# Eight-tile blocks, moves on two queues, and a new order of the first loads in a conditional residual kernel

## The chip, the cores and the metric

The kernel runs on one core of a Trainium2 chip. The metric is the device time of one execution in microseconds (us). A core has five engines with instruction streams of their own: TensorE (PE, matrix products), VectorE (DVE), ScalarE (ACT), GpSimd (POOL) and SyncE (SP, which here only starts transfers). Each works through its stream in order, and they wait for each other through semaphores. Transfers (DMA) are started by an engine's queue and carried out by 16 DMA engines beside the five.

## The reference

For x of 4 x 1024 x 512 (four rows of 1024 positions), cond of 4 x 256, W of 1536 x 512 and b of 512, all float32:

```python
hidden = concatenate([cond, cond], axis=-1)                    # 4 x 512
x_mean = mean(x, axis=1, keepdims=True)                        # 4 x 1 x 512
fused = concatenate([x, x_mean * ones_L, hidden[:, None, :] * ones_L], axis=-1)
out = x + relu(einsum('bld,do->blo', fused, W) + b)            # 4 x 1024 x 512
```

W thus has three parts of 512 rows: one is multiplied with x, one with the mean of x over a row, one with the condition. The last two and b give one vector of 512 for each row, called the bias below. It can only be finished when the whole row of x has been seen.

## The kernel before

x is cut into 32 tiles of 128 positions, eight to a row. A tile's product needs x transposed, and float32 accuracy is kept by splitting both sides into a rounded part `hi` and a rest `lo`: hi x w_hi, lo x w_hi and hi x w_lo, for each of four chunks j of 128 input columns. That is 12 products of 128x512 a tile (`product`, L565).

Row 0 is transposed by PE itself (`turn`, L329; the units in BY_PE). Rows 1 to 3 are worked in blocks of four tiles, called z4 to z9, and go another way:

- `mix` (L311): DVE transposes 32x32 squares of a loaded block, four instructions i for four tiles, into a buffer `n`.
- `shuffle` (L321): 16 transfers inside SBUF, one for each pair (i, q), carry the squares from n to their place in `z`. These are the moves inside SBUF. SP issues all of them.
- `split_hi` (L353): ACT rounds z into `hi` and sums it up beside; `split_lo` (L365): DVE or POOL takes the rest.

The bias of row r: the sums of all its `hi` give `total` (L444), four `mean_term` (L465) on DVE add up w_mean times the totals in PSUM on top of the condition's part (`weigh` L448 on ACT, `add_term` L453 on POOL), then acc_hi (L472), acc_lo (L476), and two products with a matrix of 1/L on PE, `pb` (L483), spread the sum over all partitions; `bias_copy` (L487) takes it out on ACT.

A tile ends in one of three ways. Tiles under KEEP are copied out of PSUM by ACT and get bias, relu and x later on POOL, ACT, POOL (L580, L583, L586). Others get the bias on DVE out of PSUM (L580), relu on ACT, x on POOL. Tiles from EARLY on in a row have the bias put into PSUM before the product (`preload`, L553) and need one DVE instruction at the end (L590). Then SP stores them (L595). Five PSUM banks take turns for the tiles.

The order of the work on every engine is written out before it runs by a planner (`Plan`). Each operation has a cost on each engine that may do it, dependences, and a due time; at each step the operation that can start first and is due first is taken. SEED, SPREAD and SHIFT disturb the due times. What the planner emits is fixed in the program, and so is what stands behind what on each queue. The tile framework guards the transfers of SP's queue with eight counters that take turns: a transfer is issued only when the one eight places earlier has landed.

Buffers come from pools: seven blocks of 1 MB for x and parts of W (X_BUFS), two units of `n` (N_BUFS), two of `z`, twelve pieces of `hi` and `lo`. A load of x into a buffer waits until the block that held it is finished. The first loads, SP's from 0.7 us on, are a tile of x, half of W's first part, a tile of x, the other half, and then the large ones; cond is loaded by POOL's queue after b (L253). PE transposes cond (`turn_cond`, L428) at the head of its stream.

Of the kernel before, what the change touches and what calls it, by code (L numbers as in the profile page):

```python
# [18 lines left out]
class Plan:  # L19
# [15 lines left out]
    def run(self, seed=None, spread=1.0, shift={}):  # L35
# [19 lines left out]
        while ready:  # L55
            could = []
            for key, deps in ready.items():
                costs, names, _, _, _, lag = self.ops[key]
                if deps is None:
                    deps = ready[key] = [self.done[d] for d in names if d[0] != "issued"]  # L60
                    sent = [self.done[d][0] for d in names if d[0] == "issued"]
                    self.sent[key] = max(sent, default=0.0)
                options = []
                for engine, cost in costs.items():
                    start = max(self.free[engine], self.sent[key])
                    if self.ops[key][4]:
                        start = max(start, self.landed[-self.LANES])
                    for end, by in deps:
                        start = max(start, end if by == engine else end + self.HANDOVER + lag)
                    options.append((start + cost, start, engine))  # L70
                could.append((*min(options)[1:], due[key], key))
            first = min(could)
            start, engine, _, key = min(
                (t for t in could if t[1] == first[1] and t[0] <= first[0] + self.PATIENCE),
                key=lambda t: (t[2], t[0]),
            )
            del ready[key]
            costs, _, _, _, moves, _ = self.ops[key]
            end = start + costs[engine]
            self.log.append((start, engine, key, start - self.free[engine]))  # L80
            self.free[engine] = end
            if moves:
                self.line = max(self.line, start + self.ISSUE) + moves
                self.done[key] = (self.line + self.SETTLE, None)
                self.done["issued", key] = (end, engine)
                self.landed.append(self.line + self.SETTLE)
            else:
                self.done[key] = (end, engine)
            for u in users.get(key, ()):
                missing[u] -= 1  # L90
                if not missing[u]:
                    ready[u] = None
# [9 lines left out]
def kernel(  # L102
# [20 lines left out]
    S_BUFS = 12  # L123
    O_BANKS = 5
    N_BUFS = 2
    Z_BUFS = 2
    X_BUFS = 7
    O_BUFS = 7
    KEEP, PARKED = 5, 1.4
    EARLY = (99, 14, 20, 28)  # L130
    SINGLE = 2
    TERMS = 3
    N_WARM = 5
    SEED, SPREAD, SHIFT = 4710, 1.0, {
        "z": 2.0, "turn": -5.6, "stored": -16.3, "lo": 3.7, "acc_lo": 2.1, "acc_end": -3.2,
        "relu": 1.8, "finished": -0.1, "freed": 5.6, "preload": -3.1, "bias": 1.7, "w_lo": 7.2,
        "sh": -0.2, "acc_hi": -0.3, "added": -3.1, "mix": 1.8, "total": -2.1, "turn_cond": -2.2,
        "ones": 3.6, "x": -1.0, "hi": -1.4, "sum": -4.3, "product": 2.2, "copy_cond": -1.7,
        "w_hi": -0.8, "acc": -2.1, "weigh": 0.1, "mean": -5.0, "b_row": -2.4,
    }  # L140
    STEP, START, TURN = 2.81, 5.5, 0.48
# [18 lines left out]
    plan = Plan({"pe": 1.2 + 0.43 * N_WARM, "dve": 1.3, "act": 4.3, "pool": 3.9, "sp": 3.4})  # L160
# [8 lines left out]
    units += [(r, k, G) for r in range(1, B) for k in range(0, NK, G)]  # L169
# [6 lines left out]
    for u, (r, k0, n) in enumerate(units):  # L176
        pieces += [(u, tuple(range(J)))] if n == 1 else [(u, (j,)) for j in range(J)]
    piece_of = {(u, j): c for c, (u, js) in enumerate(pieces) for j in js}
# [10 lines left out]
    c_sb = const.tile([B, H], F32, name="c_sb")  # L189
    b_sb = const.tile([P, D], F32, name="b_sb")  # L190
# [25 lines left out]
    load_w(0, slice(0, J // 2))  # L216
    load_x(0, 1, 1)
    load_w(0, slice(J // 2, J))
    table_warm = const.tile([P, 1], F32, name="table_warm")
    nc.scalar.activation(table_warm, ones, AF.Relu)  # L220
    plan.given.update({("x", 0, 0): 3.6, ("w", 0): 4.7, ("w", 1): 4.7, ("x", 0, 1): 5.4, ("w", 2): 7.2, ("w", 3): 7.2})
    plan.line0 = 6.6
    plan.landed0 = [0.0] * 4 + [3.6, 4.7, 5.4, 7.2]
# [13 lines left out]
    for v in LOADS:  # L237
        if v == ("w_mean",):
            load(v, MB, [], -9, lambda e, _: load_w(1))
        elif v == ("cond",):  # L240
            load(v, MB, frees[v], -9, lambda e, _: load_cond())
        elif v == ("x", 0):
            load(("x", 0, 2), MB / 2, [], -9, lambda e, _: load_x(0, 2, 2))
        else:
            paced = [("mix", unit_of[divmod((v[1] - 2) * G, NK)], i) for i in range(NQ)] if v[1] > 3 else []
            load(v, MB, frees[v] + paced, -9 if v[1] < 4 else at(v[1] * G) - 22, lambda e, _, g=v[1]: load_x(g))
# [6 lines left out]
    nc.gpsimd.dma_start(out=c_sb, in_=cond)  # L253
# [39 lines left out]
    for j in range(J):  # L293
        plan.add(("w_hi", j), {"dve": 0.46} if not j else {"act": 0.65}, [("w", j)], 3 + 0.7 * j,
                 lambda e, _, j=j: split_w_hi(e, j))
        plan.add(("w_lo", j), {"dve": 0.72}, [("w_hi", j)], 4 + 0.7 * j,
                 lambda e, _, j=j: nc_of[e].tensor_tensor(
                     w_lo[:, j, :], w_x[:, j, :], w_hi[:, j, :].bitcast(F32), ALU.subtract))
# [7 lines left out]
    def mix(u, i):  # L306

        r, k0, n = units[u]
        if u not in ns:
            ns[u] = npool.tile([P, NQ, n * J * Q], F32, tag="n", name=f"n{u}")  # L310
        nc.vector.transpose(  # L311
            ns[u][:, i].rearrange("p (k j t) -> p k j t", k=n, j=J),
            xs[first_tile[u] // G][:, k0 % G : k0 % G + n].rearrange("p k (j i c) -> p i k j c", j=J, i=NQ)[:, i],
        )

    def shuffle(e, u, i, q):

        if u not in zs:
            zs[u] = zpool.tile([P, NQ, G * J * Q], F32, tag="z", name=f"z{u}")
        m = units[u][2] * J * Q  # L320
        nc_of[e].dma_start(out=zs[u][i * Q : (i + 1) * Q, q, :m], in_=ns[u][q * Q : (q + 1) * Q, i, :m])  # L321

    def turn(c):
        u, js = pieces[c]
        n = units[u][2]
# [8 lines left out]
    def turned(c):  # L334
        u, js = pieces[c]
        n = units[u][2]
        if u in BY_PE:
            return xT[c][:, : n * len(js) * P]
        v = zs[u][:, :, : n * J * Q].rearrange("p q (k j t) -> p j k q t", k=n, j=J)
        return v[:, js[0]]  # L340

    def like(c, v):
        u, js = pieces[c]
        v = v[:, : units[u][2] * len(js) * P]
        return v if u in BY_PE else v.rearrange("p (k q t) -> p k q t", q=NQ, t=Q)

    def split_hi(c):
        u, js = pieces[c]
        r = units[u][0]
        s = units_of_row[r].index(u)  # L350
        hi[c] = spool.tile([P, G * P], F32R, tag="hi", name=f"hi{c}")
        lo[c] = spool.tile([P, G * P], F32R, tag="lo", name=f"lo{c}")
        nc.scalar.activation(  # L353
            like(c, hi[c]), turned(c), AF.Copy,
            accum_out=sums[:, r, js[0], s : s + 1] if len(js) == 1 else None,
        )

    def add_up(c):
        u, js = pieces[c]
# [4 lines left out]
    def split_lo(e, c):  # L364
        nc_of[e].tensor_tensor(like(c, lo[c]), turned(c), like(c, hi[c]).bitcast(F32), ALU.subtract)  # L365

    SHUFFLE = {"sp": 0.45}
    PAIRS = ((0, 0), (2, 2), (0, 1), (2, 3), (0, 2), (2, 0), (0, 3), (2, 1))
    ring = []
    for n, u in enumerate(by_z):  # L370
        r, k0, m = units[u]
        early = min(at(first_tile[u]), at(EARLY[r]) - 5)
        room = [("sh", by_z[n - N_BUFS], i, q) for i in range(NQ) for q in range(NQ)] if n >= N_BUFS else []
        into = [("lo", c) for c in range(len(pieces)) if pieces[c][0] == by_z[n - Z_BUFS]] if n >= Z_BUFS else []
        for s, i in enumerate((0, 2, 1, 3)):
            plan.add(("mix", u, i), {"dve": 0.17 * m + 0.02}, [("x", first_tile[u] // G)] + room, early - 14 + 0.9 * s,
                     lambda e, _, u=u, i=i: mix(u, i))
        for s in range(2):
            for v, (i, q) in enumerate(PAIRS):
                plan.add(("sh", u, i + s, q), SHUFFLE, [("mix", u, i + s)] + into, early - 12 + 3.6 * s + 0.45 * v,  # L380
                         lambda e, _, u=u, i=i + s, q=q: shuffle(e, u, i, q), moves=0.055 * m, lag=0.3)
    for c, (u, js) in enumerate(pieces):
        r, k0, n = units[u]

        ahead = max(0.0, at(first_tile[u]) - at(EARLY[r]) + 1.2 + 3.4 + 0.4 * js[0])
        need = (at(first_tile[u]) if u > 1 else 4.5 + 2 * first_tile[u]) + 0.7 * js[0]
# [17 lines left out]
        if c >= S_BUFS:  # L404
            v, js_v = pieces[c - S_BUFS]
            deps.append(("product", first_tile[v] + units[v][2] - 1, js_v[-1]))
# [5 lines left out]
        if u not in BY_PE:  # L412
            costs = {"dve": 0.2 + 0.14 * w, "pool": 0.1 + 0.33 * w}
        plan.add(("lo", c), costs, [("hi", c)], need - 2.2 - ahead * 0.5, lambda e, _, c=c: split_lo(e, c))
# [35 lines left out]
    def add_term(r, n):  # L450
        if not n:
            conds[r] = small.tile([P, D], F32, tag="cond", bufs=B, name=f"cond{r}")
# [48 lines left out]
    for r in range(B):  # L501
        need = at(EARLY[r]) - 1.2
        for j in range(J):
            deps = [key for c, (u, js) in enumerate(pieces) if units[u][0] == r and j in js
# [4 lines left out]
        for n in range(KH):  # L509
            i = order.index((r, n))  # L510
            deps = [("add_cond", n), ("copy_cond",), ("b_row",)] + ([("term", *order[i - TERMS])] if i >= TERMS else [])
            if i:
# [42 lines left out]
    def product(t, j, h=None, some=range(3)):  # L555
        r, k = divmod(t, NK)
        u = unit_of[r, k]
        p = piece_of[u, j]
        c = pieces[p][1].index(j) * units[u][2] + k - units[u][1]
# [38 lines left out]
    for i, (t, h) in enumerate(halves):  # L598
# [11 lines left out]
        for j in range(J):  # L610
            c = piece_of[u, j]
# [67 lines left out]
```

## Time and profile before

| what | value |
|---|---|
| median of 3 runs | 136.48 us (135.6 to 136.68) |
| the profiled execution | 136.09 us, of which 134.3 us are the span from the first to the last instruction |
| mean granted clock of PE | 0.936 |
| PE busy | 107.7 us (80%), 454 instructions |
| DVE, ACT, POOL busy | 72.8 (54%), 56.0 (42%), 61.8 us (46%) |
| moves inside SBUF | 96 of 64 KB, 2.0 us from issue to landing |
| loads of x | 7 of 1 MB, 8.5 us to landing; 2 of 256 KB, 3.5 us; 1 of 512 KB, 6.8 us |
| chain that ended last | SP's queue 24%, PE 22%, DMA 20%, DVE 19% |

The times come from one profiled execution. An engine's name with a q (SPq) is its instruction sequencer, which is where the issue of a transfer shows. In the groups of instructions a row gives line, engine, operation and tiles, then the busy time, the mean of one, and the idle time of the engine just before them with what ended it. The 40 slices are 3.36 us long each, and their digits are tenths.

### The profile page before, as it was taken

What the parts mean: (1) busy time and instruction counts of PE and PEld (TensorE: products, weight loads), DVE (VectorE), ACT (ScalarE), POOL (GpSimd) and SP (SyncE); (2) the same over time, 40 slices, a digit from 0 to 9 for tenths busy, and PEclk for the clock granted to TensorE, in tenths of its full rate; (3) what the DMA queues carried; (4) which work ended last, traced back from release to release, by engine and by line L of the source; (5) the groups of instructions that cost most, each with busy time, mean ns of one, the idle gap of its engine ahead of it and who ended that gap; (6) DMA issues with size and microseconds to landing.
All of it is one profiled execution on the core that took longest, in us unless ns stands there. A gap on an engine that the chain in (4) does not pass through costs nothing.

```text
span 134.3 us, 1590 instructions
## 1 busy us (share of the span) xinstructions
PE 107.7 (80%) x454; PEld 84.3 (63%) x454; DVE 72.8 (54%) x127; ACT 56.0 (42%) x128; POOL 61.8 (46%) x56
## 2 busy tenths in 40 slices
PE   6039999999999970069999992999980999699990
PEld 1038888878868850057778881788750687488780
DVE  1026949994098029998199059882220907772230
ACT  4006377765296057040786071672002507186000
POOL 7140070999239974925369568068000007408600
PEclk9999999999999999555999999589999689999999
DMA  3999994144493459576566688974458750002841
GB/s 126 339 391 390 389 386 173 39 100 111 94 364 98 111 150 312 148 234 216 153 210 195 211 282 274 397 237 101 107 191 276 245 147 16 0 0 79 328 158 62
DMA packets 15288, 26.32 MB, mean 196 GB/s; under 512 B 2348, under 2 KB 2608, under 8 KB 15280
## 3 DMA queue, kind: packets, MB, share of 16 engines
q1 hardware_dynamic: 15216, 26.22, 60.4%
q8 instruction: 3, 0.05, 0.2%
q14 instruction: 5, 0.04, 0.1%
q0 software_dynamic: 64, 0.01, 0.0%
HBM read 11.54 MB, written 8.39 MB: 148 GB/s over the span
## 4 chain that ended last, share of the span: by engine, by line
SPq 24%; PE 22%; DMA 20%; DVE 19%; issue 6%; POOL 3%; ACT 3%; DVEq 0%; ACTq 0%; POOLq 0%
SPq L321 20%; PE po_None L565 16%; DMA z<-n 11%; DVE acc L465 6%; DVE lo L365 5%; DVE n L311 5%; DMA x<-in_x_dram 5%; DMA c_sb<-in_cond_dram 4%; SPq L595 4%; PE xT L329 2%; ACT hi L353 2%; PE po L565 2%; POOL o L586 1%; PE pb L483 1%; PE pw L259 1%
## 5 line engine op out<-in xcount | busy, mean ns | idle before, releaser
L565 PE MATMUL po_None<-w_hi,hi 128*128 128x512 f32 x124 | 51.6, 419 | 4.0 <-ACT hi L353 4.0
L565 PE MATMUL po_None<-w_hi,lo 128*128 128x512 f32 x124 | 51.2, 415 | 0.3 <-DVE lo L365 0.2
L565 PE MATMUL po_None<-w_lo,hi 128*128 128x512 f32 x124 | 50.9, 414 | 0.0
L586 POOL TENSOR_TENSOR o<-o,x 128x512 f32<-128x512 f32 x22 | 29.2, 1350 | 21.6 <-ACT o L583 21.0
L565 PEld LDWEIGHTS po_None<-w_hi,hi 128*128 128x128 f32 x124 | 25.1, 203 | 10.8 <-ACT hi L353 4.4
L353 ACT ACTIVATE hi<-z 128x512 fp32r<-128x512 f32 x24 | 14.8, 620 | 35.6 <-DMA z<-n 35.6
L565 PEld LDWEIGHTS po_None<-w_hi,lo 128*128 128x128 f32 x124 | 24.6, 198 | 6.9 <-DVE lo L365 1.1
L565 PEld LDWEIGHTS po_None<-w_lo,hi 128*128 128x128 f32 x124 | 24.7, 199 | 5.9
L365 DVE TENSOR_TENSOR lo<-z,hi 128x512 fp32r<-128x512 f32 x17 | 15.1, 932 | 13.3 <-ACT hi L353 13.3
L365 POOL TENSOR_TENSOR lo<-z,hi 128x512 fp32r<-128x512 f32 x7 | 8.8, 1288 | 20.9 <-ACT hi L353 20.9
L311 DVE STREAM_TRANSPOSE n<-x 128x512 f32<-128x512 f32 x24 | 15.2, 681 | 1.0 <-DMA x<-in_x_dram 1.0
L583 ACT ACTIVATE o<-o 128x512 f32<-128x512 f32 x22 | 13.0, 622 | 6.1 <-DVE o L580 6.0
L590 DVE SCALAR_TENSOR_TENSOR o<-po_None,x 128x512 f32<-128x512 f32 x9 | 6.1, 689 | 11.4 <-PE po_None L565 9.2
L580 DVE TENSOR_TENSOR o<-po_None,bias 128x512 f32<-128x512 f32 x17 | 11.0, 676 | 1.9 <-ACT bias L487 1.7
L483 PE MATMUL pb<-acc_hi,mean 128*128 128x512 f32 x4 | 2.2, 548 | 12.3 <-DVE acc_lo L476 12.3
L465 DVE SCALAR_TENSOR_TENSOR acc<-w_mean,tot,acc 128x512 f32<-128x512 f32 x15 | 11.3, 753 | 0.5
L444 DVE TENSOR_REDUCE tot<-sums 128x1 f32<-128x4 f32 x16 | 2.4, 150 | 14.9 <-ACT hi L353 14.9
L353 ACT ACTIVATE hi<-xT 128x512 fp32r<-128x512 f32 (+1 forms) x10 | 5.1, 510 | 12.7 <-PE xT L329 12.7
L483 PEld LDWEIGHTS pb<-acc_hi,mean 128*128 128x128 f32 x4 | 0.8, 212 | 13.6 <-DVE acc_lo L476 13.6
L580 POOL TENSOR_TENSOR o<-o,bias 128x512 f32<-128x512 f32 x5 | 6.9, 1396 | 5.0 <-ACT bias L487 5.0
L365 DVE TENSOR_TENSOR lo<-xT,hi 128x512 fp32r<-128x512 f32 (+1 forms) x10 | 5.6, 582 | 3.3 <-ACT hi L353 3.3
L453 POOL TENSOR_TENSOR cond<-b_sb,term 128x512 f32<-128x512 f32 x4 | 5.2, 1301 | 3.6 <-ACT term L448 3.6
(51 smaller groups left out, 82.8 us busy)
## 6 DMA issues: line engine op xcount, KB each, us to landing
out_dram<-o SPq DMA_DIRECT2D x31, 256.0 KB, 2.2
x<-in_x_dram SPq DMA_DIRECT2D x7, 1024.0 KB, 8.5
z<-n SPq DMA_DIRECT2D x96, 64.0 KB, 2.0
w_x<-in_L_cond_W_dram SPq DMA_DIRECT2D x2, 512.0 KB, 5.0
w_mean<-in_L_cond_W_dram SPq DMA_DIRECT2D x1, 1024.0 KB, 11.2
w_cond<-in_L_cond_W_dram SPq DMA_DIRECT2D x1, 1024.0 KB, 13.0
x<-in_x_dram SPq DMA_DIRECT2D x2, 256.0 KB, 3.5
x<-in_x_dram SPq DMA_DIRECT2D x1, 512.0 KB, 6.8
```

The lines of the kernel that those rows point to most:

```text
L311: nc.vector.transpose(ns[u][:, i].rearrange("p (k j t) -> p k j t", k=n, j=J), xs[first_tile[u] // G][:, k0 % G : k0 % G + n].rearrange("p ...
L321: nc_of[e].dma_start(out=zs[u][i * Q : (i + 1) * Q, q, :m], in_=ns[u][q * Q : (q + 1) * Q, i, :m])
L353: nc.scalar.activation(like(c, hi[c]), turned(c), AF.Copy, accum_out=sums[:, r, js[0], s : s + 1] if len(js) == 1 else None,)
L365: nc_of[e].tensor_tensor(like(c, lo[c]), turned(c), like(c, hi[c]).bitcast(F32), ALU.subtract)
L453: nc.gpsimd.tensor_tensor(conds[r], conds[r] if n else bL, terms[r, n], ALU.add)
L465: nc.vector.scalar_tensor_tensor(acc[r], w_mean[:, j, :], scale, acc[r], ALU.mult, ALU.add)
L565: nc.tensor.matmul(po, lhsT=v[p][:, c], rhs=m[:, j, cols(h)], start=(i == 0 and not preloaded(t)), stop=(i == 3 * J - 1), skip_group_check ...
L580: nc_of[e].tensor_tensor(o, o if t < KEEP else bank(t), biases[t // NK], ALU.add)
L583: nc.scalar.activation(outs[t], outs[t], AF.Relu)
L586: nc_of[e].tensor_tensor(outs[t], outs[t], x_tile(t), ALU.add)
L590: nc.vector.scalar_tensor_tensor(o_tile(t)[:, d], bank(t, h), 0.0, x_tile(t)[:, d], ALU.max, ALU.add)
L595: nc.sync.dma_start(out=ov[r, :, k, d], in_=outs[t][:, d])
```

## The change

- Row 3 is one block of eight tiles instead of two of four (WHOLE, `units`): a move carries 128 KB, and there are 16 for the eight tiles. `pieces` keep four tiles each.
- The moves may be issued by SP or ACT (`SHUFFLE`), as the planner chooses. In the emitted program SP issues 57 and ACT 23 of 80.
- `n` is four buffers of one i each, of eight tiles' size, in place of two whole units; a mix waits for the moves of the mix four before.
- cond is loaded by ACT's queue, first thing.
- W's first part is loaded in four chunks; its rounding may go to DVE or ACT.
- x has six buffers instead of seven, `lo` ten instead of twelve, the output tiles eight instead of seven, `term` two instead of three, `cond` two instead of four; `lo` pieces are begun in order.
- KEEP, EARLY, the planner's costs for the moves, its due times, SEED and SHIFT are other numbers, so the whole order is another one.

```diff
-    S_BUFS = 12
+    S_BUFS, L_BUFS = 12, 10
+    WHOLE = 3
     O_BANKS = 5
-    N_BUFS = 2
+    N_BUFS = 4
     Z_BUFS = 2
-    X_BUFS = 7
-    O_BUFS = 7
-    KEEP, PARKED = 5, 1.4
-    EARLY = (99, 14, 20, 28)
+    X_BUFS = 6
+    O_BUFS = 8
+    KEEP, PARKED = 3, 1.4
+    EARLY = (7, 12, 20, 28)
     SINGLE = 2
-    TERMS = 3
+    TERMS = 2
...
-    units += [(r, k, G) for r in range(1, B) for k in range(0, NK, G)]
+    for r in range(1, B):
+        units += [(r, k, n) for k, n in ((0, G), (G, G))] if r < WHOLE else [(r, 0, NK)]
...
+    nc.scalar.dma_start(out=c_sb, in_=cond)
...
     load_x(0, 0, 1)
-    load_w(0, slice(0, J // 2))
+    load_w(0, slice(0, 1))
     load_x(0, 1, 1)
-    load_w(0, slice(J // 2, J))
+    for j in range(1, J):
+        load_w(0, slice(j, j + 1))
...
-    nc.gpsimd.dma_start(out=c_sb, in_=cond)
...
-        plan.add(("w_hi", j), {"dve": 0.46} if not j else {"act": 0.65}, [("w", j)], 3 + 0.7 * j,
+        plan.add(("w_hi", j), {"dve": 0.46, "act": 0.65}, [("w", j)], 2 + 0.7 * j,
...
-    def mix(u, i):
+    def mix(u, i, k):
 
         r, k0, n = units[u]
-        if u not in ns:
-            ns[u] = npool.tile([P, NQ, n * J * Q], F32, tag="n", name=f"n{u}")
+        if (u, i) not in ns:
+            ns[u, i] = npool.tile([P, NK * J * Q], F32, tag="n", name=f"n{u}_{i}")
...
-            zs[u] = zpool.tile([P, NQ, G * J * Q], F32, tag="z", name=f"z{u}")
+            zs[u] = zpool.tile([P, NQ, NK * J * Q], F32, tag="z", name=f"z{u}")
         m = units[u][2] * J * Q
-        nc_of[e].dma_start(out=zs[u][i * Q : (i + 1) * Q, q, :m], in_=ns[u][q * Q : (q + 1) * Q, i, :m])
+        nc_of[e].dma_start(out=zs[u][i * Q : (i + 1) * Q, q, :m], in_=ns[u, i][q * Q : (q + 1) * Q, :m])
...
-    SHUFFLE = {"sp": 0.45}
+    SHUFFLE = {"sp": 0.63, "act": 0.65}
...
-        room = [("sh", by_z[n - N_BUFS], i, q) for i in range(NQ) for q in range(NQ)] if n >= N_BUFS else []
...
+            room = [("sh", *mixes[-N_BUFS], q) for q in range(NQ)] if len(mixes) >= N_BUFS else []
+            mixes.append((u, i))
+            for k in range(0, m, G):
+                plan.add(("mix", u, i, k), {"dve": 0.66}, [("x", (first_tile[u] + k) // G)] + room, early - 14 + 1.4 * s + k,
+                         lambda e, _, u=u, i=i, k=k: mix(u, i, k))
...
-                         lambda e, _, u=u, i=i + s, q=q: shuffle(e, u, i, q), moves=0.055 * m, lag=0.3)
+                         lambda e, _, u=u, i=i + s, q=q: shuffle(e, u, i, q), moves=0.055 * m, lag=1.0)
...
-            conds[r] = small.tile([P, D], F32, tag="cond", bufs=B, name=f"cond{r}")
+            conds[r] = small.tile([P, D], F32, tag="cond", bufs=2, name=f"cond{r}")
```

## The prediction

> **What bounds the kernel now.** I read the waits first, then the order of time on SyncE (SP), then the order of time on TensorE (PE). From the view of the waits (engine, who it waited for, us in total, times, longest):
>
> ```profile
> ACT hi L353 <- DMA z<-n: 35.6, 6, 11.9
> ...
> PE pb L483 <- DVE acc_lo L476: 12.3, 3, 8.6
> ...
> PE pt L428 <- DMA c_sb<-in_cond_dram: 5.4, 1, 5.4
> ...
> PE po_None L565 <- ACT hi L353: 4.0, 1, 4.0
> ```
>
> All six blocks of rows 1 to 3 end their wait on the moves inside SBUF (z from n). PE itself waits at the start for cond and later for `pb` (the mean product of a row, which needs the `hi` of its last block) or for `hi`. In order of time, SP is packed with those moves:
>
> ```profile
> 24.52 10.09 SPq L321 DMA_DIRECT2D z<-n  x16
> ...
> 82.63 13.52 SPq L321 DMA_DIRECT2D z<-n  x19
> ```
>
> One move takes 10.09/16 = 0.63 us of SP, 96 of them some 60 us. A move's data lands 2.0 us after issue (median in the list of issues). The chain shows when it does not:
>
> ```profile
> 47.49 0.53 SPq L196
> ...
> 48.11 6.45 DMA z<-n
> ```
>
> A move issued right behind a 1 MB load of x on the same queue landed after 6.45 us, with the load. On PE each long wait is paid twice:
>
> ```profile
> PE   6039999999999970069999992999980999699990
> ...
> PEclk9999999999999999555999999589999689999999
> ```
>
> In the 40 slices (3.36 us each) the granted clock falls to 0.5 where PE had just stood. One-by-one starts in PE's order of time are 0.23 us apart at full clock and 0.43 after a wait: some 13 matmuls after the 8.57 us wait, 8 after the 2.44 us one, 9 after the 3.97 us one, none after 1.24 us. So PE's loss is 8.57 + 2.44 + 3.97 + 0.23 + 1.24 = 16.4 us of idle time and 30 x 0.2 = 5.9 us of slow clock, beside a first product that begins only at 11.84 us. Where PE ran without a wait (12 to 48 us) nothing else held it.
>
> **The start.** cond's load moves from POOL's queue (issued at 2.83 us, behind five SP loads, landed 5.9 us later at 8.71) to the head of ACT's queue, about 0.7 us. How fast it lands there is not shown: between 2.0 us (a move) and 5.9 (its own row). I take 2.8, the first x tile's, as both are issued at once: landed at 3.5, just when PE's warm-up ends (3.49). At 5.9 it would be there at 6.6. Next in line are the loads. They move the same bytes in the same order as before, about 0.39 MB/us, so W's first chunk lands near 4.5, the next ones near 6, 7 and 8 (the second half now: 2.13 + 5.9 = 8.0), and tiles 2 and 3 of x at 2.61 + 6.8 = 9.4. ACT loses its wait: `hi` of tile 0 at pt + 1.8 = 5.3 as now, three casts of W at 0.6 each until about 9.2 (now 13.9). DVE then has w_lo x3, lo, sum at 0.65 each until 11.2. PE's transposes of tile 2, now at 14.72 with 10 products behind them, come at 9.4 with 11: **-5.3 us**, -3.8 if cond is slow. It is tiles 2 and 3 of x that are late next. The six more load issues on SP (0.46 each) lie before transfers that are queued until 22 us anyway.
>
> **The moves.** Row 3 moves eight tiles at a time: 80 moves for 96. A move of 128 KB isn't in the trace, but issue time doesn't follow size (0.58 us at 64 KB, 0.53 for stores of 256 KB and loads of 1 MB), and a 256 KB store lands in 2.2 us. So 16 x 0.6 = 9.6 us of issue go. By the emitted order ACT issues 7, 4, 2, 5 and 5 of each block's 16. ACT issues no DMA now, so the price lies between SP's shortest, 0.38, and POOL's longest, 0.76; I take 0.6: 23 x 0.6 = 14 us on an engine that is 42% busy. What stands behind each on ACT are `hi`, `bias` and the preloads of PSUM.
>
> I walk each block (PE's rate: 2.78 us a tile, 0.74 a mean product; `hi` 0.61, `mix` 0.65, `lo` on DVE 0.64, a handover 0.1).
>
> Block of tiles 8-11: x lands near 20.2, mixes end 23.5; SP's nine moves end at 26.2, ACT's last, which now stands behind acc_hi of row 0, at 27.1; data 29.1, `hi` from there, `lo` from 30.3. PE wants it at 33.3. But here POOL's three bias adds (from 30.9) run beside `lo`, and the trace shows that this costs:
>
> ```profile
> 52.81 4.66 DVE L365 TENSOR_TENSOR lo<-z,hi 128x512 fp32r<-128x512 f32 x3
> ...
> 53.55 1.71 POOL L580 TENSOR_TENSOR o<-o,bias 128x512 f32<-128x512 f32 x1
> ...
> 104.02 2.53 DVE L365 TENSOR_TENSOR lo<-z,hi 128x512 fp32r<-128x512 f32 x4 [5.97 <-ACT hi L353]
> ```
>
> 1.55 us each beside POOL, 0.63 alone. With it the third and fourth `lo` come at 36.0 and 37.5, PE waits **1.2**.
>
> Tiles 12-15: npool now holds four quarter buffers, so each mix waits for the four moves of the block before to land; the last at 29.0. SP's moves end at 34, but its last one needs the transfer counter (eight are shared in rotation) of one that ACT issues only at 34, so data at 38.6, `hi` until 41, four mean terms at 0.85 from 40.3, then a mix, a `lo` beside POOL and acc_lo: `pb` at 46.4. PE is there at 44.2: **2.2** idle, nearer to the 2.44 row with slow clock than to 1.24 without, so 9 x 0.2 = 1.8 more, half of it taken from the next wait: **0.9**.
>
> Tiles 16-19: with X_BUFS 6 the load of tiles 20-23 waits for POOL's last add to tiles 0-3 (45.6 to 47) and is issued at 48.0; three of this block's moves stand behind it on SP's queue and land with it, at 55. The mixes of that load and two more moves on ACT come first, `hi` 57.5, first `lo` 60.4; PE, 1.4 us of row 1's last products after `pb` and then four tiles on (46.4 + 0.74 + 1.4 + 11.1), wants it at 59.7: **1.0** with the second `lo`.
>
> Tiles 20-23: all moves landed at 64.8, terms until 69.8, acc_lo behind one contended `lo`, `pb` at 71.8, PE at 70.5: **1.3**.
>
> Tiles 24-31: the second load (issued 66.6, behind three stores) lands at 73.1; four mixes among DVE's evictions until 77.8, moves until 80.5 on both queues, data 82.5, first `lo` 83.8. PE wants it at 85.0: nothing. Its `pb` has 9 us of other products ahead. This takes the place of the 3.97 and 1.24 us waits.
>
> **Buffers and small edits.** With KEEP 3, EARLY from tile 7 and three more preloaded tiles, POOL loses two bias adds and three adds of x (5 x 1.35 us), ACT trades three relus (0.62) for three preloads (0.60), DVE gets as many evictions as before. POOL is at 46% and this lies under PE's products. L_BUFS 10, TERMS 2 and two `cond` buffers put waits before a `lo`, a weigh and an add that stand blocks ahead of their use: the second weigh of row 1 comes at 27 us, as late as now, the rest is not met in the walk. I take 0, at most one 1.3 us add late on POOL per row if the cover goes. The planner's costs and SHIFT only set the order, which I have used as emitted.
>
> **Sum.** 134.3 - 5.3 - 16.4 - 5.9 + 1.2 + 2.2 + 0.9 + 1.0 + 1.3 = 113.3 us of span. The profiled run takes 136.09 for 134.3, 1.8 around it: 115.1. That run lies 0.4 under the median of 136.48, so between 115 and 115.5; I say **115**.
>
> **Two rules of the notes.** The row: 16 moves took 10.09 us to issue, 2.0 to land. The Trainium skill (DMA: Bandwidth & Descriptors, "Issuing engines are not separate DMA queues") says that a second issuing engine saves only the sequencer's issue time, usually small beside the DMA. Here issue is the large part; by the rule's "small" the move to ACT would give nothing. The Trainium skill (Perfetto Trace Analysis, "DMA Instruction — HWDGE (DVE, Sync)") also has the issuers share one descriptor generator under a lock. The trace has one issuer, so it can't tell; by it the two queues would take turns, which is the first rival.
>
> **Rivals.** (1) SP and ACT don't issue side by side. Then ACT's moves come one after SP's, at 0.6: the five blocks are 4.2, 2.4, 1.2, 3.0 and 3.0 us later. Slack takes 2.4 of the first and 1.2 of the last, which leaves 1.8 + 2.4 + 1.2 + 3.0 + 1.8 = 10 us if none of it overlaps, and 6 if a block's wait gives the next one time, as the middle three can: 119 to 123 of span, **121 to 125 us**. For it: issue time doesn't follow size, so it is a fixed cost somewhere. Against: 0.53 us of it may be SP's own. (2) The waits I add vanish: PE runs from 9.4 on as it does from 12 to 48. 134.3 - 27.6 = 106.7, **108.5 us**. Against: the two `pb` chains of 4 x 0.85 us, which nothing shortens. (3) Slower: a move on ACT must wait for its transfer counter, whose last user can be an x load (6.5 us); behind it all `hi`, `bias` and preloads stand. If that hits each of the four later blocks, 4 x 6.5 = 26 us come back: 139 of span, **141 us**. It decides from 5.3 us of PE idle per block. Against: in the emitted order the counters of x loads are met on ACT at three places, and I find the load landed or within 1 us there.
>
> **How the numbers follow.** My walk 0.66; (1) 0.18; (2) 0.08; (3) 0.05; the last 0.03 is a gain mostly eaten by several of these. The walk's own spread: the start 0 to +1.5, ACT's issue at 0.38 to 0.76 a move (-3 to +2), three waits each 1 us off: 111 to 119. To hold 8 in 10 the range goes up into the first rival and down toward the second: **110 to 123**. Under 1% can't be told from no change here (the three times lie 0.8% apart): faster 0.93, same 0.02, slower 0.05.
>
> **What would show it.** Right: first product near 6 us and the transposes of tile 2 near 9.4; no wait of PE over 3 us after 12 us; "ACT hi <- DMA z" far under 35.6; moves on ACT at 0.5 to 0.7 overlapping SP's in time. Wrong: moves of over 1 us on both queues when both issue; PE waiting on a preload or bias behind a move of ACT; the load of tiles 20-23 issued after 50 us.

## The result and the profile after

| | before | after |
|---|---|---|
| time, us | 136.58 (135.6 to 137.15) | 122.14 (121.27 to 123.51) |
| ratio | | 0.893 [0.884, 0.901] |
| span of the profiled execution | 134.3 | 121.4 |
| PE's lost time, 0 to 10 us | 6.5 | 3.4 |
| PE's lost time, from 10 us on | 24.9 | 15.9 |
| last matmul starts at | 130.5 | 117.9 |

The change is worth 14.4 us; the forecast of 115 gave it 21.5. Ratios, and the differences between kernels given below, leave out executions over 1.5% above a kernel's fastest; the profiled executions of after (123.51 us), e1, e8 and e11 are such ones, so their waits are a little on the large side. "Lost time" is used through this document: the sum, over successive matmuls, of what lies between their starts beyond the 0.235 us of full clock (gaps up to 0.27 left out). It holds idle time and slow clock together. Last matmul less lost time is 99.1 us before and 98.6 after: what changed is PE's lost time, and little else.

The waits of after (engine, who it waited for, us in total, times, longest):

```profile
ACT hi L364 <- DMA z<-n: 12.0, 4, 4.5
...
PE pb L503 <- DVE acc_lo L496: 8.7, 2, 5.8
...
ACT o L606 <- DMA x<-in_x_dram: 6.1, 1, 6.1
```

`hi` waits 12.0 us for moves where it waited 35.6. The third row is new: something on ACT's queue waits for a load of x. PE in order of time, its idle times after 6 us:

```profile
6.43 1.09 PE L338 MATMUL xT<-ident,x 128*128 128x128 f32 x4 [1.04 <-DMA x<-in_x_dram]
...
32.09 0.50 PE L588 MATMUL po_None<-w_hi,hi 128*128 128x512 f32 x1 [0.68 <-ACT po_None L575]
...
47.86 0.80 PE L503 MATMUL pb<-acc_hi,mean 128*128 128x512 f32 x1 [2.92 <-DVE acc_lo L496]
...
79.57 0.80 PE L503 MATMUL pb<-acc_hi,mean 128*128 128x512 f32 x1 [5.77 <-DVE acc_lo L496]
```

```profile
PE   6789999999799982999999993079999999999990
...
PEclk9999999999999997559999999855999999999999
```

Two holes are left, before `pb` of row 1 and of row 2, each with its slow clock behind it (slices of 3.04 us). With the clock, row 1's costs 6.0 us (40 to 60 us) and row 2's 8.4 (70 to 90). The larger one, in the chain:

```profile
58.92 0.39 SPq L205
...
59.44 8.44 DMA z<-n
...
67.89 0.51 SPq L331
...
71.69 2.06 DMA z<-n
```

At 58.92 SP issues the 1 MB load of tiles 24 to 27. A move of tiles 20 to 23 issued right behind it lands 8.44 us later, with the load. Seven moves follow the load on the two queues; the eighth is issued only at 67.69, by ACT, when it has landed, as eight counters in turn would have it, and `pb` follows at 79.57. The two queues side by side, one line each of SP and of ACT for tiles 8 to 11, then for tiles 20 to 23 (of ACT its last move):

```profile
21.22 6.67 SPq L331 DMA_DIRECT2D z<-n  x9
...
59.44 12.85 SPq L331 DMA_DIRECT2D z<-n  x11
```

```profile
22.04 4.89 ACTq L331 DMA_DIRECT2D z<-n  x6
...
67.69 0.51 ACTq L331 DMA_DIRECT2D z<-n  x1
```

The first block is issued by both in 6.7 us (10.1 for 16 before); eleven moves of the other keep SP for 12.85 us, about half of it standing.

### The profile page after: what moved, and what is told of

Same layout as the page of the kernel before. It is cut to its first block, busy times and chain, and to the rows that moved or that the text cites. A ratio compares the mean times of both kernels' runs of the same rounds, so it can differ in the third digit from the quotient of the medians.

```text
span 121.4 us, 1576 instructions
## 1 busy us (share of the span) xinstructions
PE 106.6 (88%) x451; PEld 84.0 (69%) x451; DVE 75.3 (62%) x128; ACT 55.0 (45%) x126; POOL 56.6 (47%) x51
## 4 chain that ended last, share of the span: by engine, by line
PE 32%; DMA 14%; DVE 5%; SPq 5%; issue 1%; POOL 1%; DVEq 0%
PE po_None L588 28%; DMA z<-n 9%; DMA x<-in_x_dram 5%; SPq L331 4%; DVE acc L485 2%; PE po L588 2%; PE pb L503 1%; DVE n L321 1%; POOL o L609 1%; DVE lo L377 1%; SPq L618 1%; DVE acc_lo L496 1%; DVE o L613 0%; SPq L205 0%; DVE tot L464 0%
## 5 line engine op out<-in xcount | busy, mean ns | idle before, releaser
L609 POOL TENSOR_TENSOR o<-o,x 128x512 f32<-128x512 f32 x19 | 24.8, 1334 | 20.4 <-ACT o L606 16.2
L321 DVE STREAM_TRANSPOSE n<-x 128x512 f32<-128x512 f32 x24 | 16.4, 697 | 12.3 <-DMA z<-n 12.0
L364 ACT ACTIVATE hi<-z 128x512 fp32r<-128x512 f32 x24 | 14.8, 620 | 16.4 <-DMA z<-n 12.0
L377 POOL TENSOR_TENSOR lo<-z,hi 128x512 fp32r<-128x512 f32 x8 | 10.3, 1305 | 16.4 <-DMA out_dram<-o 9.9
L377 DVE TENSOR_TENSOR lo<-z,hi 128x512 fp32r<-128x512 f32 x16 | 15.8, 1020 | 0.0
L613 DVE SCALAR_TENSOR_TENSOR o<-po_None,x 128x512 f32<-128x512 f32 x12 | 8.1, 678 | 12.0 <-PE po_None L588 10.2
L606 ACT ACTIVATE o<-o 128x512 f32<-128x512 f32 x19 | 10.9, 617 | 8.4 <-DMA x<-in_x_dram 6.1
L603 DVE TENSOR_TENSOR o<-po_None,bias 128x512 f32<-128x512 f32 x16 | 10.2, 676 | 5.2 <-ACT bias L507 4.2
L575 ACT ACTIVATE po_None<-bias 128x512 f32<-128x512 f32 x12 | 7.1, 596 | 2.5 <-DVE n L321 1.7
L473 POOL TENSOR_TENSOR cond<-cond,term 128x512 f32<-128x512 f32 x4 | 5.5, 1370 | 4.2 <-ACT term L468 3.9
L459 POOL TENSOR_TENSOR wc<-w_cond 128x512 f32<-128x512 f32 x2 | 2.5, 1286 | 10.3 <-DMA w_cond<-in_L_cond_W_dram 10.3
```

What stands on the lines that cost most here:

```text
L321: nc.vector.transpose(ns[u, i][:, k * J * Q : (k + G) * J * Q].rearrange("p (k j t) -> p k j t", k=G, j=J), xs[(first_tile[u] + k) // G].r ...
L364: nc.scalar.activation(like(c, hi[c]), turned(c), AF.Copy, accum_out=sums[:, units[u][0], js[0], s : s + 1] if len(js) == 1 else None,)
L473: nc.gpsimd.tensor_tensor(conds[r], conds[r] if n else bL, terms[r, n], ALU.add)
L575: nc.scalar.activation(bank(t, h), biases[t // NK][:, cols(h)], AF.Copy)
L603: nc_of[e].tensor_tensor(o, o if t < KEEP else bank(t), biases[t // NK], ALU.add)
L606: nc.scalar.activation(outs[t], outs[t], AF.Relu)
```

## The experiments

Each row gives the median of the kernel's four runs, the median of those that the ratio uses, the ratio to the kernel before on the same chip, the lost time from 10 us on, and when PE starts `pb` of rows 1 and 2. Differences between kernels below are of the second median. e1, e2 and e5 share a chip with a0; e3, e4, e6 and e7 share another; e8, e9 and e10 a third; e11 ran on a fourth.

| | us | us, ratio's runs | ratio | lost from 10 us | pb row 1 | pb row 2 |
|---|---|---|---|---|---|---|
| after | 122.14 | 121.83 | 0.893 [0.884, 0.901] | 15.9 | 47.86 | 79.57 |
| a0 unchanged | 123.25 | 123.25 | 0.912 [0.905, 0.920] | 16.4 | 47.93 | 79.35 |
| e1 moves on SP | 128.09 | 127.64 | 0.943 [0.932, 0.954] | 21.1 | 53.98 | 84.00 |
| e2 cond on POOL | 123.29 | 122.32 | 0.904 [0.892, 0.916] | 12.7 | 49.07 | 78.03 |
| e3 W in halves | 121.12 | 120.70 | 0.890 [0.883, 0.897] | 15.3 | 47.95 | 77.47 |
| e4 moves halved | 126.11 | 125.70 | 0.926 [0.917, 0.934] | 18.2 | 48.00 | 77.01 |
| e5 load behind moves | 120.97 | 120.96 | 0.891 [0.881, 0.900] | 11.7 | 47.71 | 73.41 |
| e6 three loads on POOL | 120.65 | 120.47 | 0.885 [0.875, 0.894] | 12.5 | 48.27 | 76.68 |
| e7 two loads behind moves | 123.60 | 123.60 | 0.912 [0.905, 0.920] | 15.4 | 45.18 | 78.94 |
| e8 e5, half on ACT | 125.67 | 124.00 | 0.913 [0.902, 0.923] | 19.4 | 48.82 | 78.14 |
| e9 two loads on POOL | 120.01 | 119.06 | 0.877 [0.869, 0.884] | 13.3 | 47.80 | 76.24 |
| e10 e9, half on ACT | 124.25 | 124.25 | 0.913 [0.905, 0.920] | 17.3 | 47.06 | 75.34 |
| e11 also tiles 16-19 on POOL | 123.75 | 121.06 (one run) | none | 16.9 | 51.17 | 81.20 |

The changed kernel's own ratio differs by 0.02 between two chips (after and a0), so differences of 2 us between chips are not read. Within one chip, and in the profiles, less than that can be.

### a0: the changed kernel again

> The changed kernel again, as it is, for a comparison on the same chip and for a second profile. Expected: 121.3 to 122.5 us; PE's wait for pb of row 2 near 5.8 us again if it comes from the order of the queues, near 1.3 us (my walk) if it was a chance of the first profile.

No edit. 123.25 us. Its profile has the two holes of after at the same places (3.08 us at 47.93, 6.18 at 79.35), so they belong to the program.

### e1: all moves on SP

```diff
-        nc_of[e].dma_start(out=zs[u][i * Q : (i + 1) * Q, q, :m], in_=ns[u, i][q * Q : (q + 1) * Q, :m])
+        nc.sync.dma_start(out=zs[u][i * Q : (i + 1) * Q, q, :m], in_=ns[u, i][q * Q : (q + 1) * Q, :m])
```

> All 80 moves are issued by SP, in the same order; nothing else differs. If the second issuing queue is what fills PE's waits (my reading): the blocks come 7, 4, 2, 5 and 5 x 0.6 us later, 6 to 10 us in all, 128 to 132 us. If the two queues take turns anyway, or the loads of x and not the issue bound the moves (rival): 121 to 123.5 us, and the moves on SP are as far apart as the two queues' were together.

128.09 us, 4.4 above a0, where 6 to 10 were expected. SP and a PE wait of this kernel in order of time:

```profile
22.02 11.03 SPq L331 DMA_DIRECT2D z<-n  x16
...
33.77 13.44 SPq L331 DMA_DIRECT2D z<-n  x19
```

```profile
37.27 0.50 PE L588 MATMUL po_None<-w_hi,hi 128*128 128x512 f32 x1 [4.23 <-ACT po_None L575]
```

The block of tiles 8 to 11 takes SP 11.03 us where both queues took 6.7, `hi` comes late, and PE waits 4.23 us where a0 waited 1.3. So 23 moves on ACT are worth 4.4 us. In after the two queues issue side by side: SP at 25.39 us for 0.59, ACT at 25.59 for 0.69, SP at 26.02 for 0.59. The first rival, that they take turns, is refuted, and of a lock between them (the Trainium skill, Perfetto Trace Analysis, "DMA Instruction — HWDGE (DVE, Sync)") these rows show 0.1 us at most: over the profiles of after and the experiments, SP's moves issued inside one of ACT's issues take 0.59 us in the median, as the others do. The Trainium skill (DMA: Bandwidth & Descriptors, "Issuing engines are not separate DMA queues") calls the time that a second issuer saves usually small beside the DMA; with transfers that land 2.0 us after issue and take 0.6 us to issue it was about 4% of the time.

### e2: cond loaded by POOL's queue; e3: W's first part in two halves

```diff
-    nc.scalar.dma_start(out=c_sb, in_=cond)
...
+    nc.gpsimd.dma_start(out=c_sb, in_=cond)
```

```diff
-    load_w(0, slice(0, 1))
+    load_w(0, slice(0, J // 2))
     load_x(0, 1, 1)
-    for j in range(1, J):
-        load_w(0, slice(j, j + 1))
+    load_w(0, slice(J // 2, J))
```

> cond is loaded by POOL's queue behind b again; nothing else differs. By my reading PE starts at 8.9 again and all that follows shifts by the 3.4 us between the two transposes of cond that remain of the start's gain: 124.5 to 126.5 us. Rival: the start is hidden, since later waits (pb of rows 1 and 2 behind the x loads) end at times that the start does not set: 121 to 123 us.

> The changed kernel with the first part of W loaded in two halves again, as in the kernel before, instead of chunk by chunk; cond stays at the head of ACT's queue. Theory, the start is hidden: PE starts its early products 1 to 2 us later, but the waits for pb of rows 1 and 2 end with the moves and get shorter by as much; 122.5 to 124, as the changed kernel on the same chip (123.25). Rival, the step of my sum that gave the start 5.3 us, of which the chunks were a part: 1.5 to 2 us more at the end, 124.7 to 125.3.

e2: 123.29 us, nothing above a0 (0.9 below); the rival of its expectation held. PE in order of time:

```profile
7.28 0.34 PE L448 MATMUL pt<-ident,c_sb 4*128 4x4 f32 x2 [3.79 <-DMA c_sb<-in_cond_dram]
...
49.07 0.70 PE L503 MATMUL pb<-acc_hi,mean 128*128 128x512 f32 x1 [2.56 <-DVE acc_lo L496]
...
78.03 0.79 PE L503 MATMUL pb<-acc_hi,mean 128*128 128x512 f32 x1 [4.22 <-DVE acc_lo L496]
```

PE transposes tile 2 at 13.21 us (a0 9.91) and starts `pb` of row 0 at 31.71 (28.56). Of these 3.2 us 1.1 are left at row 1: the wait near 32 us is gone (1.3 in a0) and the one before `pb` is shorter, because it ends with the moves. This is read from one pair of profiles. The 1.3 us by which row 2 is then early are not cond's doing: in e4, whose program is a0's up to row 3, `pb` of row 2 came at 77.01 against 79.35. That place varies by some 2 us from run to run.

e3: 121.12 us, no loss. PE transposes tile 2 at 9.53 us, a0 at 9.91, after at 10.92; over all profiles with an unchanged start it is 9.31 to 11.65. The loading of W chunk by chunk brought nothing that these runs show.

### e4: row 3's moves in two pieces each

```diff
-        nc_of[e].dma_start(out=zs[u][i * Q : (i + 1) * Q, q, :m], in_=ns[u, i][q * Q : (q + 1) * Q, :m])
+        for a in range(0, m, G * J * Q):
+            nc_of[e].dma_start(out=zs[u][i * Q : (i + 1) * Q, q, a : a + G * J * Q],
+                               in_=ns[u, i][q * Q : (q + 1) * Q, a : a + G * J * Q])
```

> The changed kernel with each of row 3's 16 moves of 128 KB issued as two of 64 KB: the same bytes, 16 more issues at 0.6 us, 11 of them on SP and 5 on ACT. Theory, issue time is what row 3's block costs: its moves end 5 to 6.6 us later, hi of tile 24 (93.09 us in the changed kernel, PE wants it near 94) with them, so PE waits 4 to 6 us there: 127 to 129.5. Rival, the wait behind loads and stores covers the issues: 123 to 124.5.

126.11 us, 5.0 above e3 on the same chip, where 4 to 6 above the changed kernel were expected. From `pb` of row 2 to `pb` of row 3 it takes 28.8 us, a0 24.3; PE waits 1.58 us for `hi`, where 4 to 6 were expected. SP's moves, and PE's wait:

```profile
75.28 16.99 SPq L332 DMA_DIRECT2D z<-n  x21
```

```profile
94.54 0.51 PE L592 MATMUL po_None<-w_hi,hi 128*128 128x512 f32 x1 [1.58 <-ACT hi L368]
```

The same bytes in 16 more issues cost 4.4 us here, 0.28 us for each, the standing on counters included (21 moves keep SP for 16.99 us, 0.81 each): PE loses 3.9 in all between 90 and 100 us, with the slow clock, where a0 loses nothing. Fewer, larger moves are worth about half of the 9.6 us of issue time that the prediction counted for them.

### e5: the load of tiles 24 to 27 behind the moves of tiles 20 to 23

```diff
     plan.run(SEED, SPREAD, SHIFT)
+    behind(lambda k: k == ("x", 6), lambda k: k[:2] == ("sh", 7))
+    behind(lambda k: k[0] == "mix" and k[1] == 8 and k[3] == 0, lambda k: k == ("acc_lo", 2))
     plan.emit()
```

`behind` takes the operations of its first argument out of the emitted order and puts them after the last of its second.

> SP issues the load of tiles 24-27 behind the moves of tiles 20-23 instead of ahead of them, and DVE does its four mixes of them behind acc_lo of row 2; nothing else differs. Theory: the 5.8 us wait for pb of row 2 comes from moves that stand behind that load, on the queue and by its transfer counter. Then hi of tiles 20-23 starts 6 to 8 us earlier, the wait falls under 1.5 us and the slow clock after it goes: 114 to 117 us. Rival: the wait is set by DVE and POOL work (lo beside POOL, four mean terms): 120.5 to 123 us.

120.97 us, 2.3 below a0: the gain is there, and less of it than expected. SP, then PE, in order of time:

```profile
58.62 7.37 SPq L331 DMA_DIRECT2D z<-n  x11
66.09 0.53 SPq L205 DMA_DIRECT2D x<-in_x_dram  x1
```

```profile
73.41 0.51 PE L503 MATMUL pb<-acc_hi,mean 128*128 128x512 f32 x1 [0.75 <-DVE acc_lo L496]
79.21 0.50 PE L588 MATMUL po_None<-w_hi,hi 128*128 128x512 f32 x1 [1.37 <-ACT po_None L575]
...
90.61 0.50 PE L588 MATMUL po_None<-w_hi,hi 128*128 128x512 f32 x1 [2.04 <-ACT hi L364]
```

Eleven moves take SP 7.37 us instead of 12.85, and `pb` of row 2 comes 5.9 us earlier with 0.75 us of idle time instead of 6.18. The edit also changes DVE's order, but the moves alone account for the gain: SP issues the last of them 6.1 us earlier than in a0 (65.40, 71.46), and ACT starts `hi` of them 6.0 us earlier (67.61, 73.62). That settles the cause of the larger hole. Then row 3 gives part back: its two loads are now late (issued at 66.09 and 68.75, the second landed at 77.2), and PE waits 1.37 and 2.04 us for what hangs on them.

### e6 and e9: loads of x issued by POOL

```diff
-        nc.sync.dma_start(out=xs[g][:, i : i + n], in_=xv[r, :, k + i : k + i + n, :])
+        (nc.gpsimd if g in (5, 6, 7) else nc.sync).dma_start(out=xs[g][:, i : i + n], in_=xv[r, :, k + i : k + i + n, :])
```

That is e6; in e9 the list is (6, 7).

> The changed kernel with the 1 MB loads of tiles 20 to 31 (three loads) issued by POOL instead of SP, behind POOL's own adds: they no longer stand on SP's queue, nor share a counter with the moves. Theory, the moves of tiles 20 to 23 were late because of queue and counters: they are issued and land without a stop, the 6 us wait for pb of row 2 falls under 2 us, 117 to 120. Rival, the 1 MB transfer itself takes the DMA engines, whoever issues it: the moves still land with it, 122 to 125.

> As e6, but only the two loads of tiles 24 to 31 go to POOL; the load of tiles 20 to 23 stays on SP, where it landed 6.1 us after issue (in e6, from POOL, 9.8). Theory, what made row 2's pb late is the load of tiles 24 to 27 ahead of the moves on their queue and in their counters: those moves start near 56.5 us instead of 61 in e6 and land with no stop, pb of row 2 comes at 72 to 74 us (79.4 in the changed kernel) and PE waits under 1.5 us for it; 117 to 119.5. Rival, the 1 MB of that load fills the engines beside the moves: pb at 77 or later, 121 to 123.

e6: 120.65 us, 0.2 below e3 on the same chip; e9: 120.01, the lowest time of the study. The interval of e9's ratio, [0.869, 0.884], lies below a0's, just below after's, and touches e3's; by the ratios its gain on the changed kernel is 1.8% (against after) to 3.9% (against a0). What the load of tiles 24 to 27 does to moves that are issued while it is under way stands in the lists of issues (KB each, median us to landing), of a0 from 58.4 to 63 us, where SP has issued it, then of e9 from 55 to 60, where POOL has:

```profile
z<-n SPq DMA_DIRECT2D x4, 64.0 KB, 8.1
z<-n ACTq DMA_DIRECT2D x3, 64.0 KB, 7.6
```

```profile
x<-in_x_dram POOLq DMA_DIRECT2D x1, 1024.0 KB, 7.6
z<-n SPq DMA_DIRECT2D x3, 64.0 KB, 5.6
z<-n ACTq DMA_DIRECT2D x1, 64.0 KB, 6.2
```

and of e9 from 63.2 to 72 us, when it has landed:

```profile
z<-n SPq DMA_DIRECT2D x7, 64.0 KB, 2.1
z<-n ACTq DMA_DIRECT2D x4, 64.0 KB, 2.0
```

Moves that are issued under the load land late on either queue, and so they do when POOL has issued it; after it they land in 2.0. One mix waits 2.80 us for such a move in e9. In after, a0, e2, e3, e4 and e9 alike, SP issues the last move of tiles 20 to 23 between 4.0 and 4.2 us after this load has landed (in after, a0 and e4 the landing is taken from the next issue, which waits for it). What e9 gains is that its load goes out and lands sooner: issued at 55.03 and landed at 62.61, in a0 at 58.50 and near 67.4. So the theory that the moves land without a stop once the load is off their queue is refuted, and the rival is right in its mechanism, the transfer itself holds the moves whoever issues it, though `pb` at 76.24 and 120.01 us lie below its figures. That the queue or the counters add to it on their own is not shown.

`pb` of row 2 comes 2.8 us later than in e5 (76.24, 73.41), without a wait before it and with 1.17 and 0.68 us ahead of it, at 63.85 and 65.03. Half of the 2.8 us are the moves, whose issue ends at 67.37 instead of 65.99; the rest is DVE's, which does the four mixes of tiles 24 to 27 (2.48 us from 68.38) ahead of the mean terms, where e5 had put them behind.

e6 shows one thing more. The load of tiles 20 to 23, issued by POOL at 49.93, ended DVE's wait at 59.77; from SP it landed after 6.2 to 7.0 us in the other kernels. A second load, issued by POOL at 55.92, ran beside its last part. ACT's queue, its engine and PE:

```profile
60.52 0.51 ACTq L331 DMA_DIRECT2D z<-n  x1
```

```profile
61.08 0.60 ACT L575 ACTIVATE po_None<-bias 128x512 f32<-128x512 f32 x1 [6.35 <-DVE n L321]
```

```profile
61.73 0.50 PE L588 MATMUL po_None<-w_hi,hi 128*128 128x512 f32 x1 [2.10 <-ACT po_None L575]
```

A move on ACT waited for the mix of that load; the preload (L575) behind it on ACT's stream waited 6.35 us with it, and PE 2.10 for the preload, which does not need the load at all.

### e7 and e11: the load of tiles 16 to 19 too

e7 adds to e5:

```diff
+    behind(lambda k: k == ("x", 4), lambda k: k[:2] == ("sh", 5))
+    behind(lambda k: k[0] in ("mix", "sh") and k[1] == 6 and k in early, lambda k: k == ("acc_lo", 1))
```

(`early`: what stood before acc_lo of row 1.) e11 is e9 with the list (4, 6, 7).

> The changed kernel with two loads put behind the moves that they stand before: the load of tiles 24 to 27 as in e5 (behind the moves of tiles 20 to 23, its mixes behind acc_lo of row 2), and the load of tiles 16 to 19 behind the moves of tiles 12 to 15, its first mixes and moves behind acc_lo of row 1. Theory, a load ahead of moves is what makes pb late in row 1 too (2.9 us idle and 2.6 us of slow clock): pb of row 1 comes 1 to 3 us earlier, 118 to 120, against 121.0 with the one load moved. Rival, row 1 is held by the work of DVE and POOL (each 8.3 of 10 us busy at 40 to 50 us): the same 120.5 to 121.5, or up to 124 where tiles 16 to 19 come late.

> As e9, with the load of tiles 16 to 19 on POOL too, so that it stands ahead of no move of tiles 12 to 15. Theory, that load makes row 1's pb late as the other makes row 2's: pb of row 1 comes at 45 to 46.5 us (47.8 in e9, 45.2 in e7) and most of the 3 us that PE waits there goes; 118 to 119.5 against e9's 120.0. Rival, the block's later tiles or the work of DVE and POOL take the gain back: pb of row 1 within 0.7 us of 47.8, or a longer wait of PE after it, 119.7 to 122.

e7: 123.60 us, 2.9 above e3 on the same chip. `pb` of row 1 comes at 45.18 with no wait, 2.5 us before e5's, and `hi` of the moves before it starts 2.7 us earlier (37.98, 40.67): a load ahead of the moves was behind the hole in row 1 as well. But the later blocks come late in turn. The load of tiles 20 to 23 is issued at 54.19 instead of 48.86, and its move on ACT holds the preload as in e6, for longer:

```profile
62.83 0.80 PE L588 MATMUL po_None<-w_hi,hi 128*128 128x512 f32 x1 [5.93 <-ACT po_None L575]
```

e11: 123.75 us (121.06 to 123.93), without an interval. Its lowest run is 2.0 above e9's median on another chip, so a gain isn't shown, and how large the loss is stays open. Here the load went out 2.9 us earlier (25.00 from POOL, 27.86 from SP in e9) and ran beside the moves of tiles 8 to 11. DVE in order of time, then PE:

```profile
31.07 0.71 DVE L321 STREAM_TRANSPOSE n<-x 128x512 f32<-128x512 f32 x1 [3.48 <-DMA z<-n]
```

```profile
32.51 0.47 PE L503 MATMUL pb<-acc_hi,mean 128*128 128x512 f32 x1 [3.10 <-DVE acc_lo L496]
```

A mix waited 3.48 us for moves, acc_lo of row 0 stood behind that mix on DVE, and PE waited 3.10 us for `pb` of row 0, which no other kernel's PE did for more than 0.7. Row 1's `pb` then had no wait but came at 51.17. The hole had moved forward by a row. Of the two theories e7's is right in its mechanism and wrong in its gain; e11's `pb` of row 1 came later, not earlier, since the load, issued by POOL, held the moves of another block.

### e8 and e10: every second move on ACT from tile 20 on

```diff
+    for u in (7, 8):
+        for n, v in enumerate([v for v in plan.log if v[2][:2] == ("sh", u)]):
+            at = [w[2] for w in plan.log].index(v[2])
+            plan.log[at] = (v[0], "act" if n % 2 else "sp", *v[2:])
```

added to e5 (e8) and to e9 (e10).

> e5 (load of tiles 24 to 27 behind the moves) with every second move of tiles 20 to 23 and of row 3 on ACT: 8 and 8 instead of 11 and 5. Theory, after e5 SP's issues set when the moves end (7.4 us for 11 of them, then 8.2 us for 10): each block ends 1.5 to 2 us earlier, and the 1.37 and 2.04 us that PE waits in e5's row 3 go; 118 to 119.5. Rival, ACT's moves wait for mixes, and hi and preloads behind them come late by as much: 121 to 123.

> e9 and e8's split together: the two loads of tiles 24 to 31 on POOL, every second move of tiles 20 to 31 on ACT. Theory, both waits that are left after row 1 (the moves behind a load, and their issue on SP) are gone: 116 to 118.5. Rival, ACT's in-order queue: a preload of PSUM behind a move that waits for its mix costs PE 2 to 6 us, as at 61.73 us in e6 and 62.83 in e7: 120 to 123.

e8: 125.67 us, 4.9 above e9 on the same chip; e10: 124.25, 5.2 above it. Both theories fell. In e8 the hole before `pb` of row 2 is back. The load of tiles 24 to 27 stands behind SP's moves, but one of ACT's is issued after it, at 65.52 us against 65.41. The issues from 65.4 to 66 us, and PE:

```profile
x<-in_x_dram SPq DMA_DIRECT2D x1, 1024.0 KB, 7.1
z<-n ACTq DMA_DIRECT2D x1, 64.0 KB, 6.8
```

```profile
78.14 0.80 PE L503 MATMUL pb<-acc_hi,mean 128*128 128x512 f32 x1 [4.65 <-DVE acc_lo L496]
```

One move, 0.1 us behind the load and on the other queue, landed with it, and PE waited 4.65 us where e5's had waited 0.75. In row 3 the issues of the block end no earlier in either kernel. In e10 ACT, and PE:

```profile
81.90 6.08 ACTq L331 DMA_DIRECT2D z<-n  x5
```

```profile
92.79 0.49 PE L588 MATMUL po_None<-w_hi,hi 128*128 128x512 f32 x1 [3.48 <-ACT hi L364]
```

The last mix of row 3 is done at 82.25, but ACT's five moves behind it take until 87.98, about half of it standing; in e9, with five moves on ACT and eleven on SP, the issues end at 86.24, and `hi` of tile 24 starts at 89.72 against 92.01. Of these 2.3 us 1.2 are there before the block's first move: the last load of x landed at 77.94 instead of 76.70. Moves of 128 KB took 4.0 (SP) and 4.8 us (ACT) to land in e10, 3.3 and 3.7 in e9, and with eight counters each waits for the eighth before it. Which part of the rest is the counters' and which the slower landing was not told apart.

## Why the prediction was right in part

It forecast 115 in a range of 110 to 123; 122.14 lies at the upper end. The walk's own spread was 111 to 119, and the range went up to 123 to take in part of the first rival, which e1 refutes: that the time fell inside it is in part luck. Of the walk's signs two came, moves on ACT at 0.5 to 0.7 us beside SP's and the fall of `hi`'s wait for moves (35.6 to 12.0 us); "no wait of PE over 3 us" did not. Two queues and fewer moves did remove the old waits, as the walk said, but it missed what one load does to the moves behind it.

- **The start, -5.3 us.** cond landed as assumed (PE transposes it at 3.42, forecast 3.5). The transposes of tile 2 came at 10.92, not 9.4, so -3.8 in the profiled run (9.31 to 11.65 in others with the same start). The chunks of W had no part in it that e3 shows. And two thirds of an early start are lost again at the next wait that a move ends (e2: 3.2 us late at row 0, 1.1 at row 1); the sum carried it whole to the end.
- **The removed waits, -16.4 and -5.9.** They went as forecast: PE's lost time from 10 us on was 24.9 us, where the sum removes 22.3, and nearly all that after loses there stands in the next three points.
- **Tiles 8 to 11, +1.2, and tiles 16 to 19, +1.0.** 0.68 us at 32.09, and none at tiles 16 to 19, though the load there went out at 49.02 and landed at 55.5, as forecast (48.0 and 55).
- **Row 1's pb, +2.2 and +0.9.** 2.92 idle and 13 matmuls at 0.43: 6.0 us with the slow clock. `pb` came at 47.86 (forecast 46.4); the slow clock was counted at half, on the ground that the next wait takes the rest, and there was no next wait.
- **Row 2's pb, +1.3.** This is the step that failed: 5.77 us idle and 8.4 us of lost time instead of 1.3, which alone is as much as the 7 us that the centre was low by; the errors of the other terms nearly cancel. The step had all moves of tiles 20 to 23 landed at 64.8 us; they landed at 73.75. It does not even name the load of tiles 24 to 27 that is emitted ahead of them. That load was issued at 58.92 and landed near 67.7, and the seven moves of SP that came after it took from 67.89 to 72.28 to issue. The chain of before had shown the price (6.45 us for a move behind a load); it was charged in full to tiles 16 to 19 alone. e5 put the load behind the moves, and `pb` came 5.9 us earlier.
- **Tiles 24 to 31, 0.** Right for the changed kernel (no wait before the last `pb`), and just so: `hi` of tile 24 was there at 93.09, and in e4, e5, e7, e8 and e10 PE waited there, 1.58 to 3.48 us.
- **Moves on ACT, 0.6 us each.** 0.51 to 0.69 where nothing stood. The 16 issues less were worth 4.4 us where e4 put them back, not 9.6.
- **Rivals.** The first (no issuing side by side) gave the right time for the wrong reason and is refuted by e1. The second (108.5) is far off. The third, ACT's moves behind a load of x, was counted as nearly excluded; its wait happened at one block (ACT's queue stood until 67.69 us for the load, and a relu behind it waited 6.1 us), but it was SP's moves, in the same wait, that set `pb`.

What stays open: why the same load and moves land 2 us sooner in some runs (`pb` of row 2 at 77.01 in e4, 79.35 in a0), whether the queue or the counters cost anything beside the load's own transfer, and how much of e10's loss is the counters'.

## What to carry to other kernels

Small transfers that take 0.6 us to issue and 2 us to land were issue-bound here: two issuing engines (4.4 us) and larger transfers (4.4 us) both paid. Before counting the gain, list every large load in the emitted order and see which small transfers are issued while it is under way, on any queue; the moves behind one load were most of this forecast's error. An engine's stream that issues transfers also holds whatever stands behind a waiting transfer, so more of them on a second engine is not always better: here 5 of 16 was faster than 8 of 16.

## What the runs showed that was not expected

- Moves on ACT's queue landed after 7.6 us (a0) under a load on SP's queue, and after 2.0 (e5) without it. A second queue did not spare them, and neither did a load on POOL's queue (6.2, e9).
- A load of 1 MB issued by POOL took 9.8 us to release DVE (e6), the same load from SP 6.2 to 7.0; whether POOL or the second load beside it made it slow was not told apart. The issue itself kept POOL for 0.77 to 0.86 us.
- Most of a late start vanishes: 3.2 us at PE's first row were 1.1 a row later (e2).
- Repairs moved holes rather than closing them: e5's gain of 5.9 us at row 2 was 2.3 at the end, e7's of 2.5 at row 1 less than nothing. The fastest, e9, came out at 120.0.
